# Mixture of experts: 128-slot blocks with gathered weights replaced by 256-slot experts with plain loads and a shared block of rests

## The chip, the cores and the metric

The kernel runs on one core of one Trainium2 chip. TensorE (PE) multiplies, VectorE (DVE), ScalarE (ACT) and GpSimd (POOL) do the rest, and SyncE (SP), ScalarE and GpSimd issue DMA transfers. The metric is the device time of one execution in microseconds; less is better. All data is float32.

## The reference

Two layers, each an "attention" part times the Silu of a "feed-forward" part, added to the input. Layer 0 mixes its 2 x 512 tokens of 256 features with a state-space scan (the attention part) and with eight gated experts (the feed-forward part). Layer 1 is causal grouped-query attention of 32 heads and a binary-weight gate. The change touches only the experts of layer 0:

```python
def _L0_ffn_ref(x, gate_w, fc1_w, fc2_w, proj_w):     # E, K, I, C = 8, 2, 704, 256
    xt = x.reshape(-1, c)                              # 1024 tokens
    router = xt @ gate_w.T
    probs, idx = jax.lax.top_k(router, K)
    probs = jax.nn.softmax(probs, axis=-1)
    comb = jnp.einsum('nk,nke->ne', probs, jax.nn.one_hot(idx, E))
    y = jnp.zeros_like(xt)
    for e in range(E):
        h = jax.nn.silu(xt @ fc1_w[e].T) * (xt @ fc2_w[e].T)
        y = y + comb[:, e:e + 1] * (h @ proj_w[e].T)
    return y.reshape(b, t, c)
```

So 2,048 pairs of a token and an expert are to be computed. The inputs are fixed. Worked out from them, the eight experts get 259, 261, 243, 287, 247, 253, 250 and 248 tokens.

## The kernel before

One function builds the whole program; a scheduler orders each engine's instructions from the order in which they are written, except within stretches that are marked as ordered by hand. Every engine runs its own instructions strictly in that order, and so do the DMA queues of SP, ScalarE and GpSimd.

The work runs in these stages. Up to 31 us: normalise, project, route (two top-1 searches per token over eight scores, written as one-hot tables `oh1` and `oh2`). From 31 to 49 us: turn the one-hots into tables of slots. From there to about 262 us: the state-space scan of layer 0, chunk by chunk of 128 tokens (`chunk(b, i0)`: `decays`, `outputs`, `passed`, and for the first batch `gated`, `projected_out`, `scanned`), the convolutions of the second batch (`convolved`), and the experts, interleaved by hand as a list of calls (L701 to L729). Then the tail of layer 0 and the attention of layer 1, 281 us to the end, which the change doesn't touch.

Slots: an expert with n tokens gets ceil(n/128) blocks of 128 slots, laid one expert behind the other. With the counts above these are 3, 3, 2, 3, 2, 2, 2 and 2, 19 blocks together. `BLK` = 23 is the most there can be. `FEW` = 19 blocks always run; the rest stands under a branch at the end (L730 to L734) on the number of blocks used, and isn't run with these inputs. The tables say for each slot its token (`tok`), the row that its result goes to (`dest`), its weight (`wt`), and for each block its expert's row of weights (`wrow`). They are built on VectorE by sums and comparisons and, on TensorE, by multiplying one-hot tables (L419).

A block n: `inputs` (L616) gathers its 128 token rows (`xg`) and its expert's hidden weights (`w`, 11 x 256 columns, 1.4 MB) by indirect DMA from GpSimd's queue (`rows_of`, L611), and transposes the tokens (L623). `hidden` (L628) does 22 matmuls with a 128x128 piece of the weights stationary and the 128 tokens moving (L636), Silu on ScalarE, and products on VectorE. `project` (L648) does six matmuls of 256 columns (L651), scales by the slot's weight on ScalarE, and scatters the rows to `chosen` in DRAM by indirect DMA (L655). `blocks` (L661) runs three blocks staggered: the inputs of one, the hidden layer of the one before, the projection of the one before that. Two sets of weight buffers alternate between two series of blocks; a block of the same expert as the one before in its series gets an index out of bounds, so that the gather moves nothing.

Each token's two result rows are fetched from `chosen` after the last scatter (`fetched`), added and passed through Silu. PSUM is eight banks of 128 x 512: four for the experts (`bank_a`), four for the rest (`bank_b`).

Of the kernel before, what the change touches and what calls it, by code (L numbers as in the profile page):

```python
# [8 lines left out]
F32 = mybir.dt.float32  # L9
# [11 lines left out]
BLK = 2 * B * T // P + E - 1  # L21
FEW = BLK - 4
SERIES = (0, (FEW + 1) // 2), ((FEW + 1) // 2, FEW)
WID1 = 11 * KC * P
WID2 = 6 * C
BIG = 4096.0
PAIRS, KV, HD = 16, 8, 64
# [16 lines left out]
def fused_kernel(  # L44
# [7 lines left out]
    moe_w: bass.AP,  # L52
    moe_p: bass.AP,
# [89 lines left out]

    thr = const.tile([P, BLK], F32, tag="thr", name="thr")
    G.iota(thr, [[P, BLK]], base=0, channel_multiplier=0, allow_small_or_imprecise_dtypes=True)
# [4 lines left out]
    part = const.tile([P, 1], F32, tag="part", name="part")  # L150
    G.iota(part, [[0, 1]], base=0, channel_multiplier=1, allow_small_or_imprecise_dtypes=True)
    token = const.tile([P, NT], F32, tag="token", name="token")
    G.iota(token, [[P, NT]], base=0, channel_multiplier=1, allow_small_or_imprecise_dtypes=True)
# [130 lines left out]
    def top(name):  # L284
        m = rt(f"m_{name}", [NT])
        V.tensor_reduce(m, r, AX.X, ALU.max)
        oh = rt(f"oh_{name}", [NT, E])
        V.tensor_tensor(oh, r, over(m.unsqueeze(2), NT, E), ALU.is_equal)
        V.tensor_tensor(oh, oh, first, ALU.mult)
        f = rt(f"f_{name}", [NT])  # L290
        V.tensor_reduce(f, oh, AX.X, ALU.max)
        V.tensor_tensor(oh, oh, over(f.unsqueeze(2), NT, E), ALU.is_equal)
        return m, oh
# [3 lines left out]
    both = rt("both", [NT, E])  # L297
    flat = both.rearrange("p t e -> p (t e)")
    first_batch, second_batch = range(TPB), range(TPB, NT)
    with tc.manual_schedule():  # L300
# [31 lines left out]
        m1, oh1 = top("1")  # L332
        V.scalar_tensor_tensor(r, oh1, -3.0e38, r, ALU.mult, ALU.add)
        m2, oh2 = top("2")
        V.tensor_tensor(both, oh1, oh2, ALU.add)
        gates(0, range(2, NH))
        ps, ps2 = bank_b(), bank_b()
        PE.matmul(ps[:, : NT * E], lhsT=upper, rhs=flat, start=True, stop=True)
        PE.matmul(ps2[:, : NT * E], lhsT=ones, rhs=flat, start=True, stop=True)
# [3 lines left out]

    rank, before = rt("rank", [NT, E]), rt("before", [NT + 1, E])
    V.tensor_tensor(rank.rearrange("p t e -> p (t e)"), ps[:, : NT * E], flat, ALU.subtract)
    V.memset(before[:, 0, :], 0.0)
    for t in range(NT):
        V.tensor_tensor(before[:, t + 1, :], before[:, t, :], ps2[:, t * E : (t + 1) * E], ALU.add)  # L350
    over_thr = rt("over_thr", [E, NT])
    V.tensor_tensor(over_thr, over(before[:, NT, :].unsqueeze(2), E, NT),
                    over(thr[:, :NT].unsqueeze(1), E, NT), ALU.is_gt)
    nblk, ends = rt("nblk", [E]), rt("ends", [E])
    V.tensor_reduce(nblk, over_thr, AX.X, ALU.add)
    V.tensor_copy(ends[:, 0:1], nblk[:, 0:1])
    for e in range(1, E):
        V.tensor_tensor(ends[:, e : e + 1], ends[:, e - 1 : e], nblk[:, e : e + 1], ALU.add)

    past, eb = rt("past", [BLK, E]), rt("eb", [BLK])  # L360
    V.tensor_tensor(past, over(blk.unsqueeze(2), BLK, E), over(ends.unsqueeze(1), BLK, E),
                    ALU.is_ge)
    V.tensor_reduce(eb, past, AX.X, ALU.add)
    V.tensor_scalar(eb, eb, float(E - 1), None, ALU.min)

    count = rt("count", [1], mybir.dt.int32)
    V.tensor_copy(count, ends[:, E - 1 : E])


    need = rt("need", [BLK])  # L370
    V.memset(need, 0.0)
    for lo, hi in SERIES:
        V.tensor_tensor(need[:, lo + 1 : hi], eb[:, lo + 1 : hi], eb[:, lo : hi - 1], ALU.is_equal)
    V.tensor_scalar(eb, eb, float(P), part, ALU.mult, ALU.add)
    wrow = rt("wrow", [BLK], mybir.dt.int32)
    V.scalar_tensor_tensor(wrow, need, BIG, eb, ALU.mult, ALU.add)

    V.tensor_tensor(rank, rank, before[:, :NT, :], ALU.add)
    V.tensor_tensor(ends, ends, nblk, ALU.subtract)
    V.scalar_tensor_tensor(rank, over(ends.unsqueeze(1), NT, E), float(P), rank, ALU.mult, ALU.add)  # L380
# [5 lines left out]
    p1, p2 = rt("p1", [NT]), rt("p2", [NT])  # L386
    V.tensor_scalar(p1, m2, 1.0, None, ALU.add)
    V.reciprocal(p1, p1)
    V.tensor_tensor(p2, m2, p1, ALU.mult)

    tab = bank_b()
    for n, (oh, p) in enumerate(((oh1, p1), (oh2, p2))):
        V.tensor_tensor(oh, oh, rank, ALU.mult)
        sl = rt("sl", [NT])
        V.tensor_reduce(sl, oh, AX.X, ALU.add)
        past = rt("past2", [NT, BLK - 1])
        V.tensor_tensor(past, over(sl.unsqueeze(2), NT, BLK - 1),
                        over(thr[:, 1:].unsqueeze(1), NT, BLK - 1), ALU.is_ge)  # L400
        at = rt("at", [NT])
        V.tensor_reduce(at, past, AX.X, ALU.add)
        ohb = rt("ohb", [NT, BLK])
        V.tensor_tensor(ohb, over(blk.unsqueeze(1), NT, BLK), over(at.unsqueeze(2), NT, BLK),
                        ALU.is_equal)
# [836 lines left out]
```

## Time and profile before

| | us |
|---|---|
| median of 3 runs | 672.87 (671.26 to 673.3) |
| the profiled execution | 670.59 |
| its span | 668.9 |
| TensorE busy | 628.8 (94%) |
| VectorE busy | 438.7 (66%) |
| ScalarE busy | 372.3 (56%) |
| GpSimd busy | 283.2 (42%) |
| expert hidden matmuls (L636), 836 records, busy | 97.6 |
| expert projections (L651), 228 records, busy | 53.2 |

The page divides the span into 40 slices of 16.7 us and gives busy shares in tenths. "PEclk" is the TensorE clock that was granted. Further lines group instructions by the source line, the engine, the operation and the tiles (out<-in). PE is the matmul itself, PEld the load of the stationary operand. Float32 matmuls appear as two records each, transposes as one. Instructions overlap within TensorE, so the sum of their durations is more than the time they take; what one costs is read from the chain that ended last, which follows the work back from the end. Landing of a DMA is counted from its issue.

### The profile page before, as it was taken

The page shows a single profiled execution, that of the slowest core. Times are in us where ns is not written, and L with a number is a line of the kernel's source. Part 1 is how long each engine was busy: PE and PEld are TensorE (multiplying, and loading weights), DVE is VectorE, ACT ScalarE, POOL GpSimd, SP SyncE. Part 2 cuts the span into 40 slices and gives each one's busy share as a digit, 9 for nine tenths or more (in the row PEclk, how much of TensorE's full clock was granted, in tenths as well). Part 3 has the DMA queues.
Part 4 walks back from the last instruction along what each step waited for, and adds up shares of the span by engine and source line. Part 5 has one row for each costly group of instructions (what it writes and reads, how often), then busy time and mean ns, then how long its engine had stood idle before and what let it go on. Part 6 is the DMA issues. An engine that isn't in the chain of part 4 may idle for free.

```text
span 668.9 us, 11922 instructions
## 1 busy us (share of the span) xinstructions
PE 628.8 (94%) x4260; PEld 450.6 (67%) x4260; DVE 438.7 (66%) x1454; ACT 372.3 (56%) x944; POOL 283.2 (42%) x306
## 2 busy tenths in 40 slices
PE   3977899999999999899889999989999999999997
PEld 1663787889999986545455565546886666666676
DVE  7475866533422454789989996999228888888511
ACT  2524435522312241376788986968308888888710
POOL 2021333334455321145555755454305666677600
PEclk9977999999999999899999999999999999999999
DMA  5252140252445403500000000021000000000000
GB/s 187 68 219 78 50 144 25 100 193 85 166 158 174 149 16 110 182 2 1 1 1 1 1 1 1 2 71 56 8 25 1 1 1 1 1 2 1 1 2 31
DMA packets 18173, 38.84 MB, mean 58 GB/s; under 512 B 4957, under 2 KB 12895, under 8 KB 16960
## 3 DMA queue, kind: packets, MB, share of 16 engines
q0 software_dynamic: 7296, 24.66, 10.8%
q1 hardware_dynamic: 9424, 11.83, 5.4%
q10 hardware_dynamic: 1392, 1.57, 0.7%
q8 instruction: 34, 0.56, 0.3%
q14 instruction: 27, 0.22, 0.1%
HBM read 56.13 MB, written 4.59 MB: 91 GB/s over the span
## 4 chain that ended last, share of the span: by engine, by line
PE 72%; DVE 17%; DMA 5%; ACT 3%; issue 2%; POOL 1%; ACTq 0%; DVEq 0%; POOLq 0%
PE bank_a L636 10%; PE bank L935 9%; PE bank L943 8%; PE bank L923 7%; PE bank L816 7%; PE bank L884 7%; PE bank_a L651 6%; DVE pr L897 4%; DMA chosen<-o,dest 3%; PE bank_b L237 2%; PE bank_a L237 2%; DMA y<-chosen 1%; PE bank L833 1%; PE bank L795 1%; PE bank_b L595 1%
## 5 line engine op out<-in xcount | busy, mean ns | idle before, releaser
L911 POOL TENSOR_SCALAR pr<-pr,den 128x128 f32<-128x128 f32 (+2 forms) x192 | 193.6, 1024 | 153.4 <-DVE den L1099 120.3
L903 ACT ACTIVATE pr<-pr,nmax 128x128 f32<-128x128 f32 (+3 forms) x256 | 142.7, 558 | 18.8 <-DVE nmax L897 18.1
L897 DVE CUSTOM_DVE_ANT_0 pr<-bank,cmask 128x128 f32<-128x128 f32 (+3 forms) x256 | 109.9, 485 | 14.6 <-PE bank L884 14.2
L636 PEld LDWEIGHTS bank_a<-xgT,w 128*128 128x128 f32 x836 | 96.9, 192 | 1.9 <-DVE xgT L625 0.5
L636 PE MATMUL bank_a<-xgT,w 128*128 128x128 f32 x836 | 97.6, 275 | 0.3 <-DVE xgT L625 0.3
L924 ACT COPY pt<-bank 128x384 f32<-128x384 f32 (+1 forms) x192 | 84.9, 518 | 13.1 <-PE bank L923 13.1
L923 PEld LDWEIGHTS bank<-ident,pr 128*128 128x128 f32 x640 | 71.3, 141 | 24.1 <-issue 17.6
L935 PE MATMUL bank<-pt,v 128*64 128x256 f32 (+3 forms) x512 | 82.9, 443 | 0.8 <-ACT pt L924 0.8
L923 PE MATMUL bank<-ident,pr 128*128 128x128 f32 x640 | 75.7, 273 | 5.5 <-DVE oT L1083 5.2
L935 PEld LDWEIGHTS bank<-pt,v 128*64 128x64 f32 x512 | 39.2, 136 | 49.0 <-ACT pt L924 23.7
L884 PE MATMUL bank<-kT,q 64*64 64x128 f32 (+7 forms) x1024 | 69.8, 410 | 0.7 <-ACT v L835 0.7
L816 PE MATMUL bank<-x1T,w_q 128*128 128x512 f32 x124 | 61.5, 618 | 0.0
L943 PE MATMUL bank<-w_o,oT 128*128 128x256 f32 x256 | 56.1, 380 | 0.6 <-DVE oT L1080 0.6
L612 POOL DMA_INDIRECT w<-in_moe_w,wrow x19 | 20.0, 1055 | 80.8 <-PE bank_a L623 43.2
L651 PE MATMUL bank_a<-wp,hid 128*128 128x256 f32 x228 | 53.2, 380 | 0.4 <-issue 0.3
L943 PEld LDWEIGHTS bank<-w_o,oT 128*128 128x128 f32 x256 | 48.3, 190 | 7.7 <-DVE oT L1080 0.8
L903 ACT ACTIVATION_READ_ACCUMULATOR pr<-pr,nmax 128x1 f32 x256 | 49.1, 192 | 0.0
L884 PEld LDWEIGHTS bank<-kT,q 64*64 64x64 f32 x1024 | 38.0, 133 | 14.3 <-issue 5.1
L640 DVE TENSOR_TENSOR hid<-hid,bank_a 128x512 f32<-128x512 f32 x19 | 13.0, 686 | 52.8 <-PE bank_a L636 51.4
L816 PEld LDWEIGHTS bank<-x1T,w_q 128*128 128x128 f32 x124 | 21.0, 189 | 36.9 <-issue 27.0
L651 PEld LDWEIGHTS bank_a<-wp,hid 128*128 128x128 f32 x228 | 41.5, 190 | 5.5 <-issue 0.4
L909 ACT ACTIVATE pr<-pr,den 128x512 f32<-128x512 f32 x32 | 23.2, 724 | 22.4 <-DVE den L1121 22.4
(250 smaller groups left out, 849.0 us busy)
## 6 DMA issues: line engine op xcount, KB each, us to landing
w_q<-in_wq SPq DMA_DIRECT2D x2, 1024.0 KB, 10.3
w_o<-in_wo SPq DMA_DIRECT2D x2, 1024.0 KB, 7.0
rows<-xn SPq DMA_DIRECT2D x4, 256.0 KB, 2.1
xn<-chosen SPq DMA_DIRECT2D x4, 256.0 KB, 3.2
out_x<-y SPq DMA_DIRECT2D x8, 128.0 KB, 1.7
w_in<-in_in_w SPq DMA_DIRECT2D x2, 386.0 KB, 5.4
x_sb<-in_x ACTq DMA_DIRECT2D x4, 128.0 KB, 3.6
x_sb<-in_x SPq DMA_DIRECT2D x4, 128.0 KB, 3.4
```

The lines of the kernel that those rows point to most:

```text
L237: PE.matmul(ps, lhsT=w, rhs=hT[b][:, k, :], start=(k == 0), stop=(k == KC - 1))
L636: PE.matmul(banks[bank][:, i * P : (i + 1) * P], lhsT=w[:, a : a + P], rhs=xgT[:, k * P : (k + 1) * P], start=(k == 0), stop=(k == KC - 1))
L651: PE.matmul(ps[:, :C], lhsT=hid[:, j * P : (j + 1) * P], rhs=wp[:, j * C : (j + 1) * C], start=(j == 0), stop=(j == 5))
L816: PE.matmul(ps, lhsT=w[:, k, n * P : (n + 1) * P], rhs=x1T[:, k, batch(b)], start=(k == 0), stop=(k == KC - 1))
L884: PE.matmul(pss[hh][to, a : a + full], lhsT=q[half, n * HD : (n + 1) * HD], rhs=kT[b][half, m, :full], start=True, stop=True)
L897: V.tensor_tensor_reduce(w["pr"][hh][:, span(i)], w["ps"][i][hh], cmask[:, i & 1, T - (i + 1) * P :], -1.0, 3.0e38, ALU.add, ALU.min, w["n ...
L903: S.activation(x, x, AF.Exp, scale=-1.0, bias=w["nmax"][hh][:, i : i + 1], accum_out=sum_of(w, i, hh))
L911: eng.tensor_scalar(x, x, sum_of(w, i, hh), None, ALU.mult)
L923: PE.transpose(ps[:, col : col + P], pr[hh][:, at : at + P], ident)
L924: S.copy(pts[hh][:, bank_at[n] : bank_at[n] + widths[n]], ps[:, : widths[n]])
L935: PE.matmul(pv[hh * HD : (hh + 1) * HD, j * P :], lhsT=v_sb[b][:, j, g * HD : (g + 1) * HD], rhs=pts[hh][:, at : at + w], start=(j == 0), ...
L943: PE.matmul(ps[:, :C], lhsT=oTs[b][:, c, i * P : (i + 1) * P], rhs=made["w_o"][c // 8][:, c % 8, :], start=(c == 0), stop=(c == PAIRS - 1))
```

## The change

Each expert owns two blocks of 128 slots (`OWN` = 256), whether or not it has the tokens; these run as one unit, with the tokens of both blocks moving together in matmuls of 256 columns. Which weights a unit needs is known when the program is built, so SP loads them by plain DMA (`weights_of`, `last_weights_of`), two buffers for the hidden weights and one for the projection's. The weights lie in DRAM in nine pieces of 512 columns per expert.

Tokens beyond 256 of an expert go to rests of 32 slots, four rests to a block. A block of rests (`rests`) keeps the tokens stationary, 32 columns of the array for each rest, and lets that rest's expert's weights move: four matmuls with 32-column stationary operands, on the four column quarters. Its weights come piece by piece by indirect DMA, four gathers of 128 x 512 to a piece, through two buffers borrowed from tiles of the first batch that are free by then; piece i+2 is asked for once the matmuls on piece i are written. Its results are transposed for the projection. One block of rests always runs, as a generator whose steps (`next(few)`) are spread between experts 4 to 7; further ones stand under the branch. With the counts above, experts 0, 1 and 3 have 3, 5 and 31 tokens beyond 256: three rests, one block.

The tables are computed in another way, for both choices and all experts in wide instructions, with running sums by doubling; the table that the matmuls build has two values per slot instead of three. The scratch tiles of this are borrowed from the scan's.

```diff
-BLK = 2 * B * T // P + E - 1
-FEW = BLK - 4
-SERIES = (0, (FEW + 1) // 2), ((FEW + 1) // 2, FEW)
-WID1 = 11 * KC * P
+OWN = 2 * P
+REST = 32
+RPB = P // REST
+RESTS = 2 * (B * T - OWN) // REST
+BLK = 2 * E + RESTS // RPB
+MANY = 3
+PIECE = 512
+PIECES = 9
+WID1 = 4 * PIECE + 2 * 384
...
+    V.tensor_tensor(sums[0][:, ran], both[:, 1 : 1 + NT], both[:, :NT], ALU.add)
+    V.tensor_tensor(sums[1][:, ran], sums[0][:, ran], sums[0][:, 2 : 2 + NT], ALU.add)
+    V.tensor_tensor(sums[0][:, ran], sums[1][:, ran], sums[1][:, :NT], ALU.add)
...
-    for t in range(NT):
-        V.tensor_tensor(before[:, t + 1, :], before[:, t, :], ps2[:, t * E : (t + 1) * E], ALU.add)
-    ...
-    for n, (oh, p) in enumerate(((oh1, p1), (oh2, p2))):
-        ...
+    def weights_of(e):
+        w = ep.tile([P, WID1], F32, tag="w", name=f"w{e}")
+        nc.sync.dma_start(w[:, : 4 * PIECE].rearrange("p (n c) -> p n c", n=4), by_expert[e, :, :4])
+        nc.sync.dma_start(w[:, 4 * PIECE :].rearrange("p (n c) -> p n c", n=2),
+                          by_expert[e, :, 4:6, :384])
+        weights[e] = [w]
+    def last_weights_of(e):
+        wp = ep.tile([P, WID2], F32, tag="wp", name=f"wp{e}", bufs=1)
+        nc.sync.dma_start(wp.rearrange("p (n c) -> p n c", n=3), by_expert[e, :, 6:])
+        weights[e].append(wp)
+    weights_of(0)
+    last_weights_of(0)
+    rank = rt("rank", [NT, E])
+    ...
+    over_thr = lent("xe", "over_thr", E, RESTS // 2)
+    V.tensor_tensor(over_thr, over(ps[:, counted[0] : counted[1]].unsqueeze(2), E, RESTS // 2),
+                    over(thr.unsqueeze(1), E, RESTS // 2), ALU.is_gt)
+    V.tensor_reduce(nrest[0][:, 4:], over_thr, AX.X, ALU.add)
+    ...
+    ohp = rt("ohp", [2, NT, E])
+    V.tensor_tensor(ohp, chosen_by, over(at.unsqueeze(1), 2, NT, E), ALU.mult)
+    V.tensor_reduce(sl, ohp.rearrange("p n t e -> p (n t) e"), AX.X, ALU.add)
+    ...
+    V.tensor_tensor(ohb, over(blk.unsqueeze(1), 2 * NT, BLK), over(bl.unsqueeze(2), 2 * NT, BLK),
+                    ALU.is_equal)
...
-    bufs = [(ep.tile([P, WID1], F32, tag=f"w{i}", name=f"w{i}", bufs=1),
-             ep.tile([P, WID2], F32, tag=f"wp{i}", name=f"wp{i}", bufs=1)) for i in range(2)]
-    def inputs(n, w): ...
-    def hidden(n, w, xgT): ...
-    def project(n, wp, hid): ...
-    def blocks(count): ...
+    def hidden(hid, w, xgT, groups, name):
+        def into(*chunks):
+            ps = bank_a()
+            for i, (f, m) in enumerate(chunks):
+                for k in range(KC):
+                    a = chunk_at(f, m, k)
+                    PE.matmul(ps[:, i * OWN : (i + 1) * OWN], lhsT=w[:, a : a + P],
+                              rhs=xgT[:, k * OWN : (k + 1) * OWN],
+                              start=(k == 0), stop=(k == KC - 1))
+            return ps
+        for m in groups:
+            to = ep.tile([P, 2 * OWN], F32, tag="hid", name=f"hid{name}_{m}", bufs=4)
+            hid.append(to)
+            one = into((0, m), (0, m + 1))
+            S.activation(to, one, AF.Silu)
+            if m < 4:
+                two = into((1, m), (1, m + 1))
+                V.tensor_tensor(to, to, two, ALU.mult)
+            ...
+    def project(e, ws, hid):
+        wp = ws[1]
+        for i in halves_of:
+            ps = bank_a()
+            for j in range(6):
+                a = j % 2 * OWN + i * P
+                PE.matmul(ps[:, :C], lhsT=hid[j // 2][:, a : a + P], rhs=wp[:, j * C : (j + 1) * C],
+                          start=(j == 0), stop=(j == 5))
+            returned(2 * e + i, ps[:, :C], f"{e}_{i}")
+    def expert_begun(e):
+        if e == 0:
+            xgs[0] = gathered(0)
+            xgTs[0] = turned(0, xgs.pop(0))
+        if e + 1 < E:
+            xgs[e + 1] = gathered(e + 1)
+            weights_of(e + 1)
+        hid = []
+        hidden(hid, weights[e][0], xgTs[e], (0,), e)
+        if e > 0:
+            project(*ends_of.pop())
+            last_weights_of(e)
+        ends_of.append((e, weights[e], hid))
+    def expert_rest(e):
+        hid = ends_of[0][2]
+        hidden(hid, weights[e][0], xgTs[e], (2,), e)
+        if e + 1 < E:
+            xgTs[e + 1] = turned(e + 1, xgs.pop(e + 1))
+        hidden(hid, weights[e][0], xgTs.pop(e), (4,), e)
+    def rests(q):
+        n, held_by = 2 * E + q, {}
+        def quarter(g):
+            return slice(g * REST, (g + 1) * REST)
+        def load(i):
+            if i >= PIECES:
+                return
+            buf = mem.tile([P, RPB, PIECE], F32, tag=("gT0", "ssmT0")[i % 2], name=f"piece{q}_{i}")
+            for g in range(RPB):
+                rows_of(buf[:, g, :], moe, wrow[:, RPB * q + g, i : i + 1])
+            held_by[i] = buf
+        xg = ep.tile([P, C], F32, tag="xgr", name=f"xgr{q}", bufs=1)
+        slots(n, xg)
+        load(0)
+        load(1)
+        ...
+        yield
+        for f, width in ((0, PIECE), (1, PIECE), (2, 384)):
+            ps = bank_b()
+            for k in range(KC):
+                buf = held_by.pop(2 * f + k)
+                for g in range(RPB):
+                    PE.matmul(ps[quarter(g), :width],
+                              lhsT=xgT[:, k * P + g * REST : k * P + (g + 1) * REST],
+                              rhs=buf[:, g, :width], start=(k == 0), stop=(k == KC - 1))
+                load(2 * f + k + 2)
+            ...
+            yield
+        ...
+        ps = bank_b()
+        for i in range(6, PIECES):
+            buf = held_by.pop(i)
+            for j in range(2 * (i - 6), 2 * (i - 6) + 2):
+                for g in range(RPB):
+                    at = j % 4 * P + g * REST
+                    PE.matmul(ps[quarter(g), :C], lhsT=hqT[j // 4][:, at : at + REST],
+                              rhs=buf[:, g, j % 2 * C : (j % 2 + 1) * C],
+                              start=(j == 0), stop=(j == 5))
+            load(i + 2)
+            if i + 1 < PIECES:
+                yield
+        returned(n, ps[:, :C], f"r{q}")
...
     chunk(0, 0)
-    blocks(1)
+    expert_begun(0)
     chunk(0, 1)
-    blocks(1)
+    expert_rest(0)
     convolved(1, 0)
+    expert_begun(1)
...
+    few = rests(0)
+    next(few)
+    expert_begun(4)
     chunk(1, 0)
-    blocks(5)
+    expert_rest(4)
+    next(few)
+    expert_begun(5)
+    next(few)
+    expert_rest(5)
+    next(few)
     chunk(1, 1)
-    blocks(FEW - 17)
+    expert_begun(6)
+    next(few)
+    expert_rest(6)
+    next(few)
     decays(1, 2)
+    expert_begun(7)
+    next(few)
+    expert_rest(7)
+    for _ in few:
+        pass
     decays(1, 3)
-    blocks(1)
-    finished(FEW - 2)
     tc.no_sync_barrier()
-    started(FEW - 1)
-    finished(FEW - 1)
+    project(*ends_of.pop())
```

## The prediction

> **What bounds the kernel now.** I read the slices of the span first, then the stages of the expert part, then the chain that ended last, and last the groups that the change touches. The slices:
>
> ```profile
> PE   3977899999999999899889999989999999999997
> DVE  7475866533422454789989996999228888888511
> POOL 2021333334455321145555755454305666677600
> PEclk9977999999999999899999999999999999999999
> ```
>
> From slice 4 on (a slice is 16.7 us) TensorE is busy nearly throughout; VectorE and GpSimd have room until slice 16, where attention begins. The hole is slices 1 to 3, where the routing tables are made and the clock falls to 0.7. By stages (columns: length, busy time of PE, PEld, DVE, ACT, POOL, clock, DMA share, GB/s):
>
> ```profile
> 37.00:57.00 20.00, 12.44 (x69) 11.36 (x70) 14.24 (x68) 2.49 (x10) 6.42 (x6) 0.73 0.64 236
> 57.00:100.00 43.00, 40.60 (x241) 32.27 (x240) 29.71 (x69) 19.80 (x29) 11.81 (x12) 0.97 0.24 81
> 100.00:145.00 45.00, 44.22 (x283) 37.66 (x282) 25.95 (x62) 21.10 (x30) 13.99 (x13) 1.00 0.25 84
> 145.00:175.00 30.00, 30.00 (x218) 27.55 (x218) 9.85 (x21) 8.11 (x15) 15.58 (x16) 1.00 0.35 109
> 175.00:216.00 41.00, 41.00 (x303) 38.53 (x302) 12.62 (x34) 10.22 (x20) 20.06 (x20) 1.00 0.55 184
> ```
>
> Between 57 and 262 us TensorE idles some 3.3 us. TensorE time taken out there leaves the span; a wait put in there is added to it. The chain shows the price of a block (start, length, what):
>
> ```profile
> 150.06 2.59 PE bank_a L651 x12
> 152.65 4.91 PE bank_a L636 x44
> 157.78 2.59 PE bank_a L651 x12
> 160.37 4.91 PE bank_a L636 x44
> 165.50 2.59 PE bank_a L651 x12
> ```
>
> A block starts every 7.72 us: 4.91 for the hidden layer, 2.59 for the projection, 0.22 for two transposes. Each matmul leaves two records, a transpose one. A record of 128 columns costs 4.91/44 = 0.112 us, one of 256 costs 2.59/12 = 0.216: cost goes by columns, and wider moving data alone saves little.
>
> **The change, part by part. Whole experts.** The token counts in the front part make nineteen 128-slot blocks: 19 x 7.72 = 146.7 us. Now eight units, each of 22 hidden matmuls of 256 columns (44 x 0.216 = 9.50), two projections (2 x 2.59 = 5.18) and four transposes (0.43): 15.1 us, eight of them 120.9. Saved: 25.8. ScalarE and VectorE get less to do in all (per expert three 512-wide Silu instead of four to six for its blocks), so neither becomes the bound.
>
> **The block of rests on TensorE.** Three rests are filled, one short block runs, the branch is not taken. Eight transposes are 0.9 us. The quarters, if four run side by side: two pairs of 512 columns (4 x 0.43 = 1.72 each), one of 384 (1.29), six projection steps of 256 (2.59): 7.3 us. If they queue, four times that, 29.3. The trace has no 32-column tile. Nearest are the value matmuls on column halves and the scores on 64x64 quadrants:
>
> ```profile
> 515.22 2.59 PE bank L935 x15
> 517.81 2.10 PE bank L884 x28
> 519.91 1.91 PE bank L816 x4
> ```
>
> One column half of the values streams 1,280 columns twice, 2 x 1280/512 x 0.43 = 2.15 us; both halves take 2.59 together, not 4.3. The quadrants stream four times 1.94 us in 2.10. For quarters no row is near enough; the Trainium skill, "TensorEngine Tiling (Array Packing)", Tiling Modes and Theoretical Speedup, lists 128x32 as four independent tiles, up to four times the speed. By it 7.3, by the halves alone 14.6; I take 7.3, as quadrants already show four. Changing the tile shape costs: four full-array 512-wide query records take 1.91 behind the scores but 1.73 elsewhere, and the values exceed their 2.15 by 0.4. Six stretches of quarters at 0.3: 2 us. Together 0.9 + 7.3 + 2.0 = 10.2. The multiplication thus saves 25.8 - 10.2 = **15.6 us**.
>
> **The loads of the rests: a wait that the change adds.** Nine pieces of 1 MB pass through two buffers; each is four indirect gathers on GpSimd's in-order queue, and piece i+2 may start only when the matmuls on piece i are done. The issue spacing, from the timeline:
>
> ```profile
> 50.10 1.00 POOL L612 DMA_INDIRECT xg<-rows,tok  x1 [0.30 <-issue]
> 51.41 1.00 POOL L612 DMA_INDIRECT wp<-in_moe_p,wrow  x1 [0.30 <-issue]
> ```
>
> and, from the page's DMA issues (last number: median us from issue to landing):
>
> ```profile
> w<-in_moe_w,wrow POOLq DMA_INDIRECT x19, 5.3
> wp<-in_moe_p,wrow POOLq DMA_INDIRECT x19, 4.1
> xg<-rows,tok POOLq DMA_INDIRECT x19, 3.7
> ```
>
> One gather per 1.31 us, landing 3.7 to 4.1 us after its issue (128 and 768 KB; a quarter is 256 KB: 3.8). A piece takes 3 x 1.31 + 3.8 = 7.7 us from its release, the following one 5.2 more. In the built program's order, with zero at the end of the matmuls on piece 0: piece 1 (0.9), six hidden matmuls (2.6) and a projection (5.2) end at 8.8; piece 2, there since 7.9, runs to 9.7; piece 3 lands at 13.1 and ends at 13.9: **3.4 us** of wait. GpSimd's queue then has two scatters, so piece 4's gathers begin at 13.2 and land at 20.9, TensorE being there at 20.6: 0.3. Piece 5 lands at 26.1, ends at 26.8 instead of 22.3: **4.5**. Pieces 6 to 8 have 17 us of other matmuls ahead of each and are covered. Queued behind the waiting gathers are expert 7's two token gathers (needed 17 us later) and the scatters of experts 4 and 5 (read only at the end): nobody waits. Pieces 0 and 1 are issued some 25 us ahead. Sum **8.2**; at the smallest landing in the trace, 2.7, 5.9; at 6 us, 10.7.
>
> The skill's rule that speaks against this is in "TensorE: Matmul & The Clock Gate", Part 1: an idle window of some 3.4 us halves the clock until a busy window restores it. The trace agrees: after 3.15 us idle at 55 us sixteen 512-wide records take 9.06 instead of 6.92. By the rule both waits reset the clock, another 2 x 1.7 = 3.4 us. But the quarters arrive 1.31 us apart and each has 0.86 us of work, so TensorE isn't idle through: I take 0, and 3.4 for the range.
>
> **Weights on SP's queue.** An expert's 1.4 and 0.8 MB go by plain loads. Two buffers hold the first, so its load starts a whole expert ahead, 15 us or more for a copy whose gathered form lands in 5.3. The single projection buffer is refilled once the expert before has projected; the last such load has 9.5 us of matmuls over it, against 4.1. Expert 0's load follows the output weights at 17 us and has over 20 us. In SP's queue the key-weight load waits for conv features at about 60 us; behind it stands expert 2's load, needed 30 us later. Cost 0; were a load late, each us would be added. GpSimd's 38 weight gathers go and 36 piece gathers come; its total stays.
>
> **Routing.** Now the longest dependent chain is VectorE's: the table is made at 30.1 us and the slot indices exist at 48.5. The new form does all experts in few wide instructions. By the rows of like size (0.26 us a step of 64, 0.35 near 190, 0.69 for 512): three sums 0.8, matmul and rank 0.8, thresholds and sums to the rank 2.6, slot and block 2.0, the wide one-hots and values 5.0, the last table matmuls 0.9, four small steps 0.8: 12.9 against 18.2, tokens 5.3 us earlier. Not all reaches TensorE: the dt chain follows its own matmuls, and the first xgT copy stands in it on VectorE, waiting for the gather. I put conv features 1 to 3 us earlier, with six hidden matmuls and the transposes (3.0 us) done before them in the former hole: **5 us**, between 2 and 7.
>
> **Coupling.** The convolution chain on VectorE at 57 to 78 us now interleaves with 512-wide copies and multiplies: 1 us of waits, 0 to 3. The tail doesn't change: from the last projection to the first transposes of the next layer 21.8 us pass, over 19 us of matmuls with 2.84 idle, and the same scatter, fetch and normalisation follow.
>
> **Sum.** 15.6 - 8.2 + 5 - 1 = 11.4 us. Span 668.9 - 11.4 = 657.5; the profiled execution took 670.59 for its span, so 659.2. The runs' median, 672.87, lies 2.3 above that execution; on it the forecast is **661.5**. With all costs at their bad ends (15.6 - 10.7 - 3.4 + 2 - 3) 0.5 is left, so 672; with good ends (15.6 - 5.9 + 7) 16.7: 656.
>
> **Rivals.** *The pieces arrive in time.* If one POOL gather spreads better than its neighbours the waits vanish: gain 19.6, 653. For it: DMA runs at 184 GB/s at 175 to 216 us with share 0.55. Against it: the 1.31 us spacing bounds a piece at 5.2 us.
> *A load decides, and it is slower.* Place: the piece queue. If a quarter's landing is 9 us under the weights' traffic, or one piece's gathers queue behind a scatter that itself waits, each of pieces 2 to 8 costs 3 to 5 us: above 19.6 us of waits in all the change loses; six pieces at 4 give 24, 677. Against it: the slowest token gather took 7.0.
> *Quarters don't overlap.* 22 us more: 683. The halves speak against it.
> *It does little:* waits on pieces and coupling eat the gain to within 2 us: 672. This asks for nearly every bad end.
> That nothing is removed can't be: 146.7 us of block matmuls are on the path.
>
> **How the numbers follow.** Forecast 0.60 (own range 656 to 670), pieces in time 0.14, little or nothing 0.09, slow pieces 0.11, no overlap 0.06. From 651 to 672 about 8 in 10 lie. 0.3% (2 us) is about what a measurement of this kernel tells from no change: faster 0.73, same 0.09, slower 0.18.
>
> **What the profile after would show.** Hidden records of 256 columns at 0.216 us, 352 of them; quarter matmuls in stretches of 1.7 us for eight (four to a step), or 3.4 and more if they queue; TensorE waiting for piece 3 and piece 5 by 3 to 5 us each, for pieces 0, 1 and 6 to 8 not at all; first token gather near 43 us instead of 48.8; no wait on plain weights. Wrong would be: waits at every piece, a clock row at 0.7 in the rests, or TensorE idle at 60 to 80 us on VectorE or ScalarE.

## The result, and the profile after

| | runs | median us | before, beside it | ratio, 95% interval |
|---|---|---|---|---|
| changed kernel | 7 | 666.82 (663.89 to 669.92) | 671.71 | 0.9923 [0.9896, 0.995] |
| the same, measured again later | 10 | 671.02 (669.61 to 673.26) | 671.85 | 0.9999 [0.9985, 1.0013] |

The forecast was 661.5 (651 to 672). The first measurement is a gain of 4.9 us, less than half of the 11.4 expected; the second shows none. The profiled execution of the first took 663.89 us with a span of 662.2 (before: 668.9), so 6.7 us are to be explained; that of the second took 669.61 with 667.9. The ratios are formed from fast runs; of all the runs in this document two were slow, both of the kernel with the late preparation.

The first profiled execution is the fastest of the 17 of this kernel, and one of only two with a mean granted clock of 0.985 or more; the other 15 have 0.976 to 0.982 (the kernel before: 0.986 in its profile and in all 36 executions measured beside the variants). A sum worked out on it shows the change at its best.

The slices of the first execution:

```profile
PE   3988999999879999799899999989999999999997
DVE  7447856654015325789989987999228888888511
POOL 3002121172575321255465564555206666677600
PEclk9969999999999999899999999999999999999999
```

TensorE's hole at slices 1 to 3 is smaller, and the 8 and the 7 in slices 10 and 11 (a slice is 16.6 us here: 166 to 199 us) are new. By stages (length, busy time of PE, PEld, DVE, ACT, POOL, clock, DMA share, GB/s):

```profile
37.00:57.00 20.00, 16.63 (x83) 15.35 (x84) 10.02 (x42) 4.48 (x13) 5.25 (x5) 0.74 0.12 33
57.00:100.00 43.00, 43.00 (x198) 33.47 (x197) 30.61 (x67) 21.86 (x30) 6.57 (x6) 1.00 0.35 117
100.00:145.00 45.00, 45.00 (x213) 35.87 (x212) 29.14 (x65) 21.53 (x30) 14.43 (x13) 1.00 0.40 132
145.00:175.00 30.00, 30.00 (x158) 23.94 (x156) 11.53 (x25) 11.82 (x18) 14.41 (x15) 1.00 0.69 221
175.00:216.00 41.00, 33.54 (x150) 21.51 (x143) 11.61 (x29) 10.24 (x15) 23.37 (x23) 0.96 0.63 207
```

From 57 to 175 us TensorE doesn't idle at all. Nearly all that the expert part loses is lost at 175 to 216, where TensorE was busy throughout before. TensorE's timeline there (start, length, what, and in brackets the idle time before it and what ended it):

```profile
174.49 2.68 PE L798 MATMUL bank_b<-piece,xgTr 128*32 128x512 f32 x12
179.01 1.04 PE L798 MATMUL bank_b<-piece,xgTr 128*32 128x512 f32 x2 [1.84 <-DMA piece<-in_moe,wrow]
181.32 1.04 PE L798 MATMUL bank_b<-piece,xgTr 128*32 128x512 f32 x2 [1.27 <-DMA piece<-in_moe,wrow]
182.30 3.72 PE L709 MATMUL bank_a<-xgT,w 128*128 128x256 f32 x16
...
188.98 0.84 PE L798 MATMUL bank_b<-piece,xgTr 128*32 128x384 f32 x4
...
195.53 0.83 PE L798 MATMUL bank_b<-piece,xgTr 128*32 128x384 f32 x2 [3.43 <-DMA piece<-in_moe,wrow]
196.67 2.85 PE L798 MATMUL bank_b<-piece,xgTr 128*32 128x384 f32 x6 [0.31 <-DMA piece<-in_moe,wrow]
199.46 1.22 PE L568 MATMUL bank_b<-rl,ones 128*128 128x512 f32 x2
```

Pieces 2 and 3 take from 174.49 to 182.30, 7.81 us; pieces 0 and 1, which were there in time, take 1.86 (164.67 to 166.53). That is 6.0 of wait. Pieces 4 and 5 take 10.48 (188.98 to 199.46); where nothing waits, in a kernel below, the same sixteen records take 1.43. That is 9.0. Together 15.0, where 8.2 was forecast. Only 7.46 us of this are idle time in the table above (41.00 less 33.54). For the rest TensorE worked on quarters that came one at a time: two records of one quarter take 1.04 us, the eight of a whole piece 0.93 when they run side by side; and at 196 to 200 us its clock was 0.57. GpSimd's timeline tells why the pieces were late:

```profile
175.23 1.00 POOL L660 DMA_INDIRECT piece<-in_moe,wrow  x1 [0.30 <-issue]
176.54 1.02 POOL L672 DMA_INDIRECT chosen<-o,dest  x1 [0.30 <-issue]
182.45 1.00 POOL L672 DMA_INDIRECT chosen<-o,dest  x1 [4.88 <-DMA chosen<-o,dest]
183.75 1.05 POOL L660 DMA_INDIRECT piece<-in_moe,wrow  x1 [0.30 <-issue]
```

Expert 4's second scatter (the second line at L672) waits on the queue until the first one has landed; both write `chosen`, and the profile names that transfer as what ended the wait. The scattered tile itself was written by 175.1 us. The gathers of piece 4 stand behind it and start at 183.75; counted from the end of the matmuls on piece 0 (165.6), the forecast had them at 178.8.

The sum, by the prediction's terms, for the execution of 662.2 us:

| term | forecast | measured |
|---|---|---|
| multiplication saved (whole experts, less rests) | 15.6 | 16.9: units as forecast; transposes and quarters 8.9 instead of 10.2 |
| waits on pieces | -8.2 | -15.0 |
| routing and front | 5 | 4.2 |
| coupling at 57 to 145 us | -1 | +3.2: idle time of 3.2 us in before is gone |
| tail | 0 | -2.4 |
| sum | 11.4 | 6.9 (the spans differ by 6.7) |

### The profile page after: what moved, and what is told of

It reads as the page before. It is cut to its first block, busy times and chain, and to the rows that moved or that the text cites. A ratio compares the mean times of both kernels' runs of the same rounds, so it can differ in the third digit from the quotient of the medians.

```text
span 662.2 us, 11004 instructions
## 1 busy us (share of the span) xinstructions
PE 619.7 (94%) x3838; PEld 420.9 (64%) x3838; DVE 432.7 (65%) x1397; ACT 380.6 (57%) x940; POOL 277.5 (42%) x309
## 4 chain that ended last, share of the span: by engine, by line
PE 44%; DVE 14%; DMA 2%; issue 1%; POOL 1%; ACT 0%; ACTq 0%; DVEq 0%; POOLq 0%
PE bank L1114 9%; PE bank L1122 8%; PE bank L1102 8%; PE bank L995 7%; PE bank L1063 7%; DVE pr L1076 5%; DMA chosen<-o,dest 1%; PE bank L1012 1%; PE bank L974 1%; DVE sw_q L985 1%; DMA y<-chosen 1%; DVE xn L222 1%; DVE q L986 1%; POOL pr L1090 1%; PE bank_b L995 1%
## 5 line engine op out<-in xcount | busy, mean ns | idle before, releaser
L1076 DVE CUSTOM_DVE_ANT_0 pr<-bank,cmask 128x128 f32<-128x128 f32 (+3 forms) x256 | 109.8, 484 | 14.6 <-PE bank L1063 11.9
L709 PE MATMUL bank_a<-xgT,w 128*128 128x256 f32 x352 | 80.6, 380 | 0.8 <-DVE xgT L693 0.8
L709 PEld LDWEIGHTS bank_a<-xgT,w 128*128 128x128 f32 x352 | 65.1, 190 | 11.6 <-issue 2.2
L660 POOL DMA_INDIRECT xg<-rows,tok x16 | 17.2, 1076 | 72.2 <-DVE tok L479 42.0
L660 POOL DMA_INDIRECT piece<-in_moe,wrow x36 | 37.1, 1030 | 23.9 <-issue 9.1
L672 POOL DMA_INDIRECT chosen<-o,dest x16 | 16.6, 1038 | 66.9 <-ACT o L671 59.1
L734 PE MATMUL bank_a<-wp,hid 128*128 128x256 f32 x192 | 43.4, 379 | 0.0
L734 PEld LDWEIGHTS bank_a<-wp,hid 128*128 128x128 f32 x192 | 36.1, 190 | 4.8
```

Source lines behind the costliest of these rows:

```text
L660: G.indirect_dma_start(out=buf, out_offset=None, in_=src[:, :], in_offset=bass.IndirectOffsetOnAxis(ap=at, axis=0), bounds_check=src.shape ...
L709: PE.matmul(ps[:, i * OWN : (i + 1) * OWN], lhsT=w[:, a : a + P], rhs=xgT[:, k * OWN : (k + 1) * OWN], start=(k == 0), stop=(k == KC - 1))
L734: PE.matmul(ps[:, :C], lhsT=hid[j // 2][:, a : a + P], rhs=wp[:, j * C : (j + 1) * C], start=(j == 0), stop=(j == 5))
L1076: V.tensor_tensor_reduce(w["pr"][hh][:, span(i)], w["ps"][i][hh], cmask[:, i & 1, T - (i + 1) * P :], -1.0, 3.0e38, ALU.add, ALU.min, w["n ...
```

## The experiments

Theory A: the waits come from the piece queue, that is from two buffers and from the scatter that holds GpSimd's queue. Rival B: landings under the weights' traffic decide. Rival C: the time isn't TensorE's, and another wait takes the place of one removed. All variants start from the changed kernel.

| kernel | median us | before, beside it | ratio, 95% interval | profiled span |
|---|---|---|---|---|
| third buffer | 658.49 | 673.20 | 0.9785 [0.9764, 0.9806] | 654.2 |
| deferred scatters | 657.70 | 673.20 | 0.9766 [0.9742, 0.979] | 656.5 |
| both | 648.31 | 673.20 | 0.9628 [0.9607, 0.9648] | 649.5 |
| without rests | 637.08 | 673.20 | 0.9463 [0.9443, 0.9484] | 636.6 |
| two weight loads left out | 658.75 | 671.66 | 0.9804 [0.9782, 0.9827] | 658.6 |
| front reordered | 667.61 | 671.66 | 0.9927 [0.9896, 0.9958] | 665.9 |
| both, early projection | 652.78 | 671.66 | 0.9709 [0.9685, 0.9733] | 651.3 |
| both, early projection, front | 652.31 | 671.66 | 0.9712 [0.9692, 0.9733] | 651.6 |
| both, late preparation | 667.19 | 671.85 | 0.9906 [0.9878, 0.9933] | 660.5 |
| both, front with a copy moved | 653.04 | 671.85 | 0.9726 [0.971, 0.9743] | 650.7 |
| both, that front, late preparation | 656.80 | 671.85 | 0.9773 [0.9753, 0.9793] | 656.3 |

The first four ran together, then the next four, then the last three with the repeat of the changed kernel. "Both" is the best version; it beats the kernel before by 24.9 us and the changed one in either of its measurements.

Below, spans are compared with the first profile of the changed kernel (662.2 us), its fastest execution. The medians show larger gains, since the changed kernel's typical execution is slower than that one: from ratios of 0.9923 and 0.9999, a third buffer gains some 9 or 14 us, the deferred scatters 10 or 16, both 20 or 25.

### A third buffer

```diff
-buf = mem.tile([P, RPB, PIECE], F32, tag=("gT0", "ssmT0")[i % 2], ...)
+if i % NBUF == 2:                       # NBUF = 3
+    buf = gT[1]                         # not written before the tail
+else:
+    buf = mem.tile([P, RPB, PIECE], F32, tag=("gT0", "ssmT0")[i % NBUF], ...)
...
-load(2 * f + k + 2)
+load(2 * f + k + NBUF)
...
```

> A third piece buffer, in space that is free until the tail, so that no gather of pieces 2 to 4 waits for the matmuls on the piece before it. Theory A (the waits come from the piece queue: two buffers, and GpSimd's queue held by a scatter that waits for the scatter before it): the wait at piece 3, 6.0 us, falls to under 0.5; piece 5 still stands behind the waiting scatter of expert 4, so a wait of 7 to 9 us is left at piece 5. Gain over the changed kernel 6 to 7 us: 660 us. Rival B (a piece's landing under the weights' traffic decides, whatever the queue does): a wait of 3 us or more stays at pieces 3 and 4, gain at most 3: 664. Rival C (TensorE isn't what sets the end here, the waits only cover another engine's work): the same waits come back elsewhere, gain under 2: 665 to 667.

The span fell by 8.0 us. TensorE's timeline:

```profile
174.71 1.07 PE L802 MATMUL bank_b<-gT,xgTr 128*32 128x512 f32 x8
175.59 1.04 PE L802 MATMUL bank_b<-piece,xgTr 128*32 128x512 f32 x8
176.56 3.72 PE L710 MATMUL bank_a<-xgT,w 128*128 128x256 f32 x16
...
183.25 0.85 PE L802 MATMUL bank_b<-piece,xgTr 128*32 128x384 f32 x8
190.59 3.44 PE L802 MATMUL bank_b<-gT,xgTr 128*32 128x384 f32 x8 [6.49 <-DMA gT<-in_moe,wrow]
```

Piece 3 waits no more; piece 5, still behind the waiting scatter, waits 6.49. That is theory A's picture. Two things are to be seen besides: the eight records after the wait take 3.44 where those of piece 4 take 0.85, because the clock at 188 to 192 us was 0.50, and the gain is 1 us or more above the 6 to 7 expected.

### Scatters behind the gathers

```diff
 def returned(n, ps, name):
     ...
-    G.indirect_dma_start(out=chosen[:, :], ...)
+    if name[0] in "45": scatters.append((n, o))
+    else: scatter(n, o)
...
 expert_begun(5)
 next(few)
+scattered()        # each issued behind the last gather of a piece
```

The same call stands behind the step after `expert_begun(6)`.

> Two buffers as in the changed kernel, but the scatters of experts 4 and 5 stand behind the gathers of the next two pieces on GpSimd's queue. Theory A: the wait at piece 3 stays at 6 us; piece 4's gathers begin near 176.5 instead of 183.8 and land before they are needed; piece 5 is released only by piece 3's matmuls and keeps 1 to 3 us of wait instead of 9.2 for both. Gain 6 to 8 us: 660. Rival B: landings of 6 us and more keep 5 us or more of wait at pieces 4 and 5, gain at most 4: 663 to 665. Rival C: gain under 2.

```profile
179.25 1.05 PE L814 MATMUL bank_b<-piece,xgTr 128*32 128x512 f32 x2 [1.72 <-DMA piece<-in_moe,wrow]
181.62 1.91 PE L814 MATMUL bank_b<-piece,xgTr 128*32 128x512 f32 x2 [1.32 <-DMA piece<-in_moe,wrow]
183.47 5.63 PE L725 MATMUL bank_a<-xgT,w 128*128 128x256 f32 x16
...
192.05 1.50 PE L814 MATMUL bank_b<-piece,xgTr 128*32 128x384 f32 x16
```

Pieces 4 and 5 are there when TensorE comes (16 records from 192.05 to 193.48 us). The wait at piece 3 stays, 6.9 us (174.74 to 183.47, less 1.86), and this time it cost more: the sixteen hidden records behind it took 5.63 us where 3.72 is usual, at a clock of 0.57 to 0.58 (180 to 188 us). So the span fell by 5.7, while the medians fell by some 10 (0.9766 against 0.9923). Theory A again; B would have left 5 us at pieces 4 and 5.

### Both

> Both edits together: third buffer, and scatters of experts 4 and 5 behind the next pieces. Theory A: waits at pieces 3 to 5 fall from 15.2 to 2 us or less; gain 13 us, 11 to 15: 653 to 655. Rival B: some 6 us of waits are left, gain 6 to 9: 659. Rival C: gain under 4: 663 or more.

The span fell by 12.7 us, the median more. TensorE's line for 175 to 216 us and its whole list of waits from 145 to 262 us:

```profile
175.00:216.00 41.00, 41.00 (x229) 31.82 (x229) 18.08 (x43) 17.44 (x24) 24.09 (x25) 1.00 0.64 215
```

```profile
PE bank_a L231 <- issue: 5.4, 1, 5.4
PE bank_b L607 <- PEq L933: 0.3, 1, 0.3
```

(The list has engine, tile and line, what ended the wait, then the sum in us, times and the longest.) No wait on a piece is left, at the same DMA share (0.64) and rate. So the queue's order and the buffers set the waits, and no other wait took their place: C is refuted.

### Without the rests

```diff
-few = rests(0)
+few = nothing()      # one scatter of zeros
```

> The block of rests is left out with its nine pieces and its matmuls (one scatter of zeros stays in its place), so the tokens beyond 256 of an expert get nothing from it. Theory A: the matmuls on quarters (8.9 us with transposes) and the waits (15.2) leave the time, 24 us: 641 to 645; no other wait takes their place. Rival C (VectorE, ScalarE or the convolution chain bound this part, or the tail's transfers do): half of it or less, 655 or more.

The span fell by 25.6 us, 1.6 above the sum of matmuls and waits. In the kernel with both edits the rests still cost 12.9 (649.5 less 636.6), their matmuls being 8.9; the other 4.0, of which 1.5 lie in the tail, are not accounted for.

### Two weight loads left out

```diff
-weights_of(e + 1)
+if e + 1 < 7: weights_of(e + 1)
+else: weights[e + 1] = [weights[e - 1][0]]
...
-last_weights_of(e)
+if e != 5: last_weights_of(e)
+else: weights[e].append(weights[e - 1][1])
```

> The changed kernel without two weight loads: expert 5's projection weights (0.8 MB, issued at 174.6 us beside the last gathers of piece 3) and expert 7's hidden weights (1.4 MB, issued at 189.1 us beside piece 5) are left out, and the tiles of expert 4 and 5 are used in their place, so the outputs of experts 5 and 7 are other numbers. The queue on GpSimd stays as it is. Theory A (queue order and buffers set the larger part of the waits, the traffic the rest): the last gather of piece 3 lands in 4 us instead of 6 and the scatter in under 3 instead of 5, so the wait at piece 3 falls from 6.0 to 3.5 to 4 and the one at pieces 4 and 5 from 9.2 to 5 to 7; gain 4 to 7 us: 660 to 663. Rival B (the traffic makes the waits): 12 us or more of the 15.2 go: 655 or less. Rival D (the traffic plays no part): gain under 2.

GpSimd's queue, as above:

```profile
176.58 1.02 POOL L672 DMA_INDIRECT chosen<-o,dest  x1 [0.30 <-issue]
180.32 1.00 POOL L672 DMA_INDIRECT chosen<-o,dest  x1 [2.71 <-DMA chosen<-o,dest]
```

The second scatter now waits 2.71 us instead of 4.88. The wait at piece 3 is 3.8 (174.54 to 180.20), at pieces 4 and 5 7.2 (186.88 to 195.49): 11.0 together. These two were all the weight loads that SP issued between 163 and 208 us, so some 4 us of the 15 are the plain loads' doing, and the rest is left to the queue and the buffers. The span fell by 3.6, a little less than theory A gave; B needed 12 of the 15 us of wait to go. The medians fell by more, some 8 us from 0.9923 and 13 from 0.9999: here the mean clock is 0.986 to 0.989 in every execution, so what the clock costs in most executions of the changed kernel is gone too.

### The changed kernel once more

> The changed kernel once more, unaltered, to see whether its runs differ by the granted clock. If the waits on pieces 3 to 5 throw TensorE's clock back in some executions and not in others, the runs with the lower mean clock are the longer ones, and a profile of such a run shows a clock well under 0.96 at 175 to 216 us with the same waits (15 us). If the spread comes from elsewhere, the stage shows 0.96 and the same busy time as before. Time 664 to 670.

The theory of the clock explains only a part. The waits at the pieces are 15.3 us as before, and the clock at 175 to 216 us is 0.87. But the order of the ten runs doesn't follow their clock (0.982 for 671.2, 0.976 for 670.63), and the profile has a wait that the first didn't have:

```profile
202.87 0.60 ACT L570 ACTIVATE ec<-bank_b 128x512 f32<-128x512 f32 x1
209.66 1.28 ACT L718 ACT_TABLE_LOAD   x1 [6.19 <-issue]
210.95 0.60 ACT L718 ACTIVATE hid<-bank_a 128x512 f32<-128x512 f32 x1
```

```profile
214.87 1.38 PE L606 MATMUL bank_b<-xe,Btok 128*128 128x512 f32 x2 [4.22 <-DVE xe L596]
```

ScalarE stands for 6.19 us ahead of a table load, and "issue" means that the profile shows nothing it waited for; its matmuls (L709, from 203.14) were ready by about 204.9. In the first profile the same place has 1.33. The scan's exponential and VectorE's `xe` are behind it, and TensorE waits 4.22 us for `xe`. The clock falls, and the scan's 18 records to 219.25 take 4.4 us instead of 2.65. These two, 5.9 us, are about the difference of the two spans (5.7). The same pause (3.51 us ahead of a table load) is in two kernels further down. In these three traces a packet of the instruction queue (q8 in the DMA view) starts 1.3 to 3.2 us ahead of the restart; in four others, without the pause, it comes 1 to 3 us behind the table load. That would fit an engine that waits for its instructions. But ScalarE also stands still ahead of a plain Silu, without a table load, in those two kernels and in a third (4.9 to 6.3 us, lines below), and no q8 packet lies near these pauses (none between 166 and 190 us, or 170 and 202). So the packets don't explain them, and the cause stays open.

### The front reordered

The dt and B projections run ahead of the table matmuls, into three banks; two features stand ahead of the gathered tokens' transposes.

```diff
+        for some in (range(3), range(3, 6), range(6, NT)):      # behind scaled(1)
+            ps3 = bank_b()
+            for j, t in enumerate(some):
+                ...PE.matmul(ps3[:, j * (NH + P) : (j + 1) * (NH + P)], ...)
...
-    for t in range(NT):
-        ps = bank_b()
-        ...
```

> Front part alone, on the changed kernel: the dt and B projections (32 records) run ahead of the table matmuls, in the hole at 36 us, into three banks instead of eight; the first two convolution features stand ahead of the gathered tokens' transposes. If the table stage was slow because TensorE came to it from a hole at half clock: the table matmuls take 3.6 us instead of 7 to 8, the first token gather is issued near 44 to 45 us instead of 47.8, and the features end 6 us or more earlier; gain 4 to 8 us: 659 to 663. Rival (the table matmuls themselves, 56 columns each, don't hold the clock, whatever runs before them): they stay at 0.22 us a record; only the order gains, 2 to 4 us. Rival (VectorE's convolution chain sets the next 20 us): TensorE idles between 50 and 80 us and the gain is under 2.

First the changed kernel, then this one, around the table matmuls:

```profile
38.59 1.38 PE L472 MATMUL bank_b<-vals,ohs 128*128 128x56 f32 x8 [2.09 <-DVE vals L464]
...
41.20 3.50 PE L472 MATMUL bank_b<-vals,ohs 128*128 128x56 f32 x16
```

```profile
32.78 3.77 PE L387 MATMUL bank_b<-w_in,hT 128*128 128x132 f32 x32
36.38 3.60 PE L257 MATMUL bank_a<-hT,w_in 128*128 128x512 f32 x8
39.95 3.75 PE L485 MATMUL bank_b<-vals,ohs 128*128 128x56 f32 x32
```

Without the hole ahead of them, and without the dt and B projections between them, the 32 table records take 3.75 us, 0.117 each, instead of 0.22. The first token gather is issued at 44.66 us (47.80), the features end at 57.06 (63.49). But the profiled span is 3.7 us longer, and the median (ratio 0.9927) is that of the changed kernel's first measurement; against its second it would be a gain of some 5 us. At 98 us TensorE waits 2.26 us for the copy of expert 2's tokens, which stands behind the scan on VectorE, and the clock makes the twelve records after it take 4.49 instead of 2.76. Piece 0 starts at 164.28, only 0.4 earlier, and the waits at the pieces cost more clock than in the first profile (0.83 at 175 to 216 us, 0.96 there). The first theory holds for the table stage. Of the third, the early features do come to nothing, by a wait for VectorE, but at 98 us and not at 50 to 80.

With that copy moved ahead of the scan's third step, on the kernel with both edits:

```diff
-chunk(0, 2)
+xgTs[2] = turned(2, xgs.pop(2))
+with tc.issue_after(copies[2].ins):      # VectorE's copy of those tokens
+    chunk(0, 2)
```

> Third buffer and deferred scatters with the reordered front, and with expert 2's token transposes and their copy on VectorE ahead of the scan's third step, where the reordered front lost 2.3 us and the clock after it. Theory (the front's 5 us were given back there, by one copy queued behind the scan on VectorE): no idle TensorE at 90 to 100 us, gain 4 to 6 us over the kernel with the two edits: 642 to 644. Rival (VectorE's work as a whole is the limit at 57 to 100 us): the idle time comes back elsewhere in 66 to 145 us and the gain stays under 2.

Piece 0 starts at 162.27 us instead of 165.15, so 2.9 us of the front are kept. They are lost again, and more, in the stretch of the pieces. First the kernel with both edits, then this one, ScalarE and TensorE:

```profile
178.86 0.60 ACT L735 ACTIVATE hid<-bank_a 128x512 f32<-128x512 f32 x1 [3.25 <-PE bank_a L726]
```

```profile
180.86 0.60 ACT L751 ACTIVATE hid<-bank_a 128x512 f32<-128x512 f32 x1 [8.13 <-PE bank_a L742]
181.51 1.13 PE L742 MATMUL bank_a<-xgT,w 128*128 128x256 f32 x4 [1.67 <-issue]
```

With both edits the Silu starts 2.03 us after its sixteen matmuls begin (176.83), here 6.91 after (173.95): ScalarE stands for 4.9 us. TensorE stops in the middle of its twelve records for 1.67 us and goes on 0.05 us after this Silu has read its bank; the profile calls the wait "issue". Then comes ScalarE's pause ahead of the table load (3.51), for which TensorE waits 4.67 us, and the cold clock behind it (1.8). Whether this front gains where the pause doesn't come is open.

### The tail

> The third buffer and the deferred scatters as before, and expert 7's last projection moved whole ahead of the last step of the scan's preparation (2 us of TensorE). Theory (the tail is a chain of transfers, from the last scatter through the fetch to the next layer's transposes, and TensorE has 4 to 5 us to spare in it): the chain starts 1.8 to 2 us earlier, gain 1.5 to 2 us over the kernel with the two edits: 646 to 647. Rival (TensorE's own work fills the tail): no gain.

```diff
+project(*ends_of.pop())
 decays(1, 3)
 tc.no_sync_barrier()
...
-project(*ends_of.pop())
```

The ratio is 0.0081 above that of both edits, some 5 us; the span is 1.8 longer. TensorE's timeline behind the branch:

```profile
235.96 2.05 PE L607 MATMUL bank_b<-xe,Btok 128*128 128x512 f32 x2 [4.20 <-DVEq L933]
```

TensorE goes on only when VectorE has reached the branch too, and VectorE comes to it when its part of the preparation is done. The projection had covered that part. The last scatter starts 1.05 us earlier (232.87 for 233.92), but TensorE ends the tail's own matmuls 5.7 us later (257.2 for 251.5), and of its idle time there 1.78 us are left (5.45).

> Third buffer and deferred scatters, and the last preparation of the scan (2.1 us of TensorE, some 5 of VectorE) moved from ahead of the last projection to behind the branch, into the tail. Theory (the tail is a chain of transfers with TensorE idle for 5.4 us in it, and the kernel that moved the projection instead lost by the 4.2 us in which TensorE stood at the branch until VectorE had finished that preparation): nothing waits at the branch, the last scatter starts 2 us earlier, TensorE's hole in the tail falls to about 3.4 us; gain 2 us over the kernel with the two edits: 646. Rival (the moved steps delay the tail's own chain on VectorE): no gain or a loss of up to 2.

```diff
-decays(1, 3)
...
-for i0 in (2, 3):
-    outputs(1, i0)
-    passed(1, i0)
+outputs(1, 2); decays(1, 3); passed(1, 2); gates(1, range(NH)); outputs(1, 3); passed(1, 3)
```

Nothing waits at the branch, and yet the span is 11.0 us longer than with both edits. In the tail the moved work costs more than it saves: from the end of the last projection to the next layer's transposes 29.3 us pass (240.4 to 269.71), instead of 24.6; 1.6 of the 4.7 are the matmuls that moved there. TensorE waits 2.14 us for `xdt` and 1.91 for `held`, the clock falls, and the 32 records of the output projection take 9.95 us (7.46). So the rival was right about the tail: VectorE's and ScalarE's part of the moved steps lies on its path.

But most of the loss lies ahead of the tail, where this edit changed nothing. The last projection ends at 240.4 us instead of 232.36, although 1.6 us of matmuls ahead of it are gone. ScalarE stands again ahead of a Silu:

```profile
187.31 0.60 ACT L735 ACTIVATE hid<-bank_a 128x512 f32<-128x512 f32 x1 [9.51 <-remote]
187.96 2.07 PE L726 MATMUL bank_a<-xgT,w 128*128 128x256 f32 x4 [3.07 <-ACT hid L735]
```

Its matmuls began at 179.01 us; with both edits the Silu would have come 2.03 us later, so it is 6.3 us late. TensorE waits 3.07 us, and the clock at 188 to 192 us is 0.50. A smaller pause before piece 0 (TensorE idle for 1.61 us at 151) makes another 2.2. The ten runs spread from 660.78 to 671.13 us. What the move alone would give is therefore not measured by the time.

> All edits together: third buffer, deferred scatters, early projection, front part reordered. If the gains add, 647 less the front's 4 to 8: 639 to 643. If the front's gain is taken up by VectorE's chain behind it, 645 or more.

> The same with the late preparation too. If both gains hold they add: 640 to 642; else the sum of what the two give alone.

("The same" is here the kernel with both edits and the front with the copy moved; the projection stays where it was.) Neither sum holds. The first shows the early projection's 4.2 us and the front's 2.3 us of waits side by side; the second the late preparation's waits (2.2 for `xdt`, 1.9 for `held`) and, again, both pauses of ScalarE (4.9 us ahead of a Silu, 3.51 ahead of a table load).

## Why the prediction held, and where its sum was wrong

The range held and the place of the waits was right, but the centre was 5.3 us too low for the first measurement and 9.5 for the second. That it was not further off is in part luck: the waits were 6.8 us longer than forecast, and the coupling, put at a loss of 1, was a gain of 3.2.

**Whole experts and quarters: right.** 352 hidden records of 256 columns take 0.216 us each in stretches (3.45 for sixteen). The quarters run side by side: sixteen records of 512 columns in 1.86 us, sixteen of 256 in 1.00. The rule of four independent column tiles, taken over the column halves' 14.6, was the right choice; the changes of shape cost 0.8 instead of 2.0.

**The loads of the rests: the step that failed.** Place and kind were right (pieces 3 to 5, none at 0 to 2 and 6 to 8). The size was 15.0 for 8.2, from two terms. "GpSimd's queue then has two scatters" counted two issues; the second waits 4.88 us for the first. The built program has that wait; the sum left it out. And a quarter was given 3.8 us to land; the last one of piece 3 took about 6. "Nobody waits" looked at who needs the scatters' data, and not at who stands behind them.

**"I take 0" for the clock: too low.** The Trainium skill, "TensorE: Matmul & The Clock Gate", Part 1, was set aside because quarters arrive singly. In the first profile that is nearly true (0.57 at 196 to 200 us, after 3.43 idle). With a third buffer 6.49 idle gave 0.50; with deferred scatters waits of 1.72 and 1.32 between short matmuls were enough, at 180 to 184 us with TensorE busy for 2.68 of 4 us. But in the first profile nearly the same bursts (waits of 1.84 and 1.27, busy for 2.73 of 4 us) kept a clock of 1.00. So short bursts hold the clock in one execution and not in another, and no run here shows what decides. Where it fell, the price was 2.6 us in the one (3.44 for 0.85) and 1.9 in the other (5.63 for 3.72), beside the wait itself. That 15 of the 17 executions have a lower mean clock than the first profile suggests that most of them paid such a price; the 3.4 us kept for the range were the better estimate.

**Weights on SP's queue "cost 0": half wrong.** TensorE never waits for a plain load, but the run without two of these loads shows that their traffic adds some 4 us to the waits for the scatter and the pieces.

**Routing: the sum was nearly right for another reason.** Tokens come 1.0 us earlier, not 5.3: VectorE was done as early as forecast (40.65 us), but the table matmuls, put at 0.9, run at half clock until 46.85. What was gained came from matmuls done early and from features at full clock.

**Coupling** was a gain of 3.2: the idle time of before at 57 to 145 us is gone. That the longer units fill it is likely, and no run tests it. **The tail** lost 2.4 us. From the end of the last projection to the next layer's transposes 24.2 us pass instead of 21.8, so a part of the 9 us by which TensorE reached it earlier was given back. TensorE waits 1.17 us at the branch for ScalarE's queue (`ACTq L911`), where before it hardly waited, and stands 4.17 us ahead of the transposes instead of 2.84.

**The rivals.** "A load decides" named the very thing that happened, a piece's gathers "queue behind a scatter that itself waits", and had the right place. It put 19.6 us as its turning point; the waits came to 15.0, so the change did not lose. "It does little" is what the second measurement shows: 15.3 us of waits, the cold clock, and a pause of ScalarE that the prediction's costs did not have.

## What to carry to other kernels

On an in-order DMA queue cost what an issue waits for, not only the issue: a scatter that waits for another scatter to the same tensor holds every load behind it, so put loads first and scatters after. Before a move, list who stands behind the moved work on every engine, at branches too: here a preparation was free only under the projection that covered it. And give a wait on the bounding engine the price of the clock after it.

## What the runs showed that was not expected

- The same program took 666.82 and 671.02 us in two measurements, while the kernel before stayed within 0.2 us (671.71 and 671.85). The profile of the second has a pause of ScalarE of 6.19 us that nothing in the profile explains, and three other kernels have pauses of 3.5 to 6.3 us, ahead of a table load or of a Silu.
- 32 records of a 128x56 table stage ran at half clock for 8 us although TensorE was busy (5.00 of 5 us at 40 to 45), after a hole of 2.09 us; without the hole, and in one stretch, they took 3.75 us.
- Indirect gathers leave GpSimd's queue every 1.30 us whatever the load; what varies is the landing: 3.4 to 7.4 us for 256 KB in the first profile, 3.8 in the middle.
